# Index tables stored as rows, transfers around a branch respaced, and the last three batches stored in natural row order

## The chip, the cores and the metric

The kernel runs on one core of a Trainium2 chip. The metric is the device time of one execution in microseconds (us), where lower is better. The time before the change is the median of three executions without the profiler; the profile is one further execution with it.

## The reference

Two layers of a graph network act on 32 batches of 512 nodes with 512 features each, all in float32. One 512x512 matrix `adj` serves all batches.

```
h = max(layernorm(x), 0)
x = x + (adj @ h) @ W0 + b0                                        # layer 0
h = max(layernorm(x), 0)
q, k, v = h@Wq+bq, h@Wk+bk, h@Wv+bv                                # layer 1, 8 heads of 64
scores = q k^T / 8 + (1 - adj) * -1e9
x = x + (softmax(scores) v) @ Wo + bo
```

The term of -1e9 outweighs the scores, so when the largest entry of a row of `adj` leads by enough, the softmax takes one neighbour only: layer 1 becomes `x[n] + (h[idx[n]] @ Wv + bv) @ Wo + bo`, where `idx[n]` is the column of the largest entry. The kernel tests for this on the chip and takes this path.

## The kernel before, in words

**Work of one batch.** A tile of x holds 512 rows as four chunks of 128 partitions. Layer 0 is an aggregation (`aggregate`) and a product with W0 (`layer0`). Layer 1 needs only the rows that some `idx` names (at most 336 of 512): the normalised rows h1 are written to a DRAM table `hs` (`put_h`), come back in packed order (`get_h` into `hc`), are multiplied by the folded weight `wvo` (`layer1`), and the result z goes to a DRAM table `z` (`put_z`). Each node then gathers its row of z and adds it to x (`finish`, an indirect DMA that accumulates), and x is stored (`store`). Large products use the seven-piece scheme in `product`, line 506 being the matmul of every piece.

**Loop and order.** `run_phase` walks over b and writes its order by hand. In loop b TensorE runs `layer0(b)`, `aggregate(b+1)` and `layer1(b-1)`; between their pieces lie 21 numbered steps, and `put(batch, step, f, ...)` hangs all other work on a step. Steps 0 to 6 belong to `layer0`, 7 to 13 to `aggregate`, 14 to 20 to `layer1`. Every engine executes its own instructions in this order. `behind` makes each indirect DMA wait until the piece before it has been taken out of PSUM.

**Queues.** Plain DMAs are issued by SyncE (SP). Every indirect DMA, gather or scatter, is issued by GpSimd (POOL). Both feed the same 16 DMA engines.

**The plan and the branch.** While loops 0 to 3 run with a full aggregation, the class `Plan` works out on the chip an order of the rows in which most of the matrix is zero in known blocks. Its steps are in `Plan.schedule`, at (loop, step). After loop 3 (`FIRST = 4`) a register is loaded from its result and all engines branch; on the path taken (`sparse`) rows of x are loaded in the new order through the index table `plan.xi`, `aggregate` becomes `spread` (matmuls of lines 618, 621 and 624), and 3 x 128 extra rows per batch are gathered (`load_g` into `plan.gx`) and normalised into `plan.HG`. That is done by `lead` for the first sparse batch and by `NormMore` (`more_stats`, line 954, and `more_relu`, line 967, on ScalarE) for the others. Rows of the first batches are in natural order (`natural(b)`), so only their `put_h` needs an indirect scatter through `dest` and only their stores are plain. All later stores scatter through `plan.xi` (line 490), each followed by a small memset on POOL (line 493).

**Three small tables in DRAM.** `places` stores `dest` (loop 1, step 0, line 581), `save_pos` stores `posi` (line 1243), `save_pi` stores `pi` (loop 6, step 4, line 1249). Each holds 512 integers that lie on chip as 128 partitions x 4 and are written as

```python
nc.sync.dma_start(table.rearrange("(c p) o -> p (c o)", p=P), dest)
```

so that each integer of 4 bytes is a run of its own in DRAM. Gathers of one integer per partition read them (`look_up`, `look_1`, `look_2`).

**The end.** Batch 31 takes no gather-and-add: `get_all` gathers h1 of every node, and `layer1_rows` transposes it (line 684, copied by ScalarE at line 685) and multiplies it row chunk by row chunk (line 696), adding into x on VectorE (line 699). z of batches 29 and 30 is fetched to spare tiles (`fetch`, into `sel` and `yT`), added on VectorE (`add_z`, line 755) and stored between these. `add_cvo` (line 688) adds the folded bias to batch 31.

Of the kernel before, what the change touches and what calls it, by code (L numbers as in the profile page):

```python
# [408 lines left out]
def single_path(ctx: ExitStack, tc: tile.TileContext, x, adj, out, kept, room):  # L409
# [13 lines left out]
    dest = consts.tile([P, C], I32, name="dest")  # L423
    place = consts.tile([P, C], I32, name="place")
# [12 lines left out]
    hs_d = [dram.tile([N, D], F32, name=f"hs{i}") for i in range(3)]  # L437
    z_d = [dram.tile([32 * S, D], F32, name=f"z{i}") for i in range(3)]
# [16 lines left out]
    def run_phase(batches, sparse, small, ps_m, ps_t):  # L455
        ordered = folded and (sparse or batches[0] == 0)

        def natural(b):
            return not ordered or b <= FIRST

# [25 lines left out]
        def store_rows(b, c, eng):  # L486
            if natural(b):
                eng.dma_start(out[b, c * P:(c + 1) * P, :], X[b][:, c, :])
                return
            stored = behind(nc.gpsimd.indirect_dma_start(  # L490
                out=out_rows, out_offset=bass.IndirectOffsetOnAxis(ap=plan.xi[:, b, c:c + 1], axis=0),
                in_=X[b][:, c, :], in_offset=None))
            nc.gpsimd.memset(gap, 0.0)  # L493
            for other_rows in stored_rows:
                tc.declare_no_dep(stored.ins, other_rows.ins, reason="other rows")
            stored_rows.append(stored)
# [81 lines left out]

        def places():
            table = dram.tile([N, 1], I32, name="table", bufs=1)  # L580
            nc.sync.dma_start(table.rearrange("(c p) o -> p (c o)", p=P), dest)
            return table
# [94 lines left out]
        def get_all(b):  # L677
            for c in range(C):
                gather(hs[0][:, c, :], hs_d[b % 3], idx[:, c, 0:1] if natural(b) else plan.pq[:, c:c + 1])
# [10 lines left out]
        def layer1_rows(b):  # L690
            for r in range(C):
                bank = ps_m.tile([P, D], F32, name="mm")
                for d in range(DC):
                    if d == 2 and r + 1 < C:
                        transpose_all(r + 1)
                    nc.tensor.matmul(bank, hs[1][:, d, r * P:(r + 1) * P], wvo[:, d, :], start=(d == 0),
                                     stop=(d == DC - 1))
                x_r = X[b][:, r, :].rearrange("p (q c e) -> p q c e", q=4, c=4)
                nc.vector.tensor_add(x_r, bank.rearrange("p (c q e) -> p q c e", q=4, c=4), x_r)
                if sparse and r == 0:  # L700
                    for c in range(C):
                        add_z(B - 3, c, nc.sync)
                    fetch(B - 2)
                store_rows(b, r, nc.sync)
                for i in range(2):
                    if not sparse:
                        add_z(B - 3 + r // 2, 2 * (r % 2) + i, nc.sync if r < 2 else nc.scalar)
                    elif 0 < r < C - 1:
                        add_z(B - 2, 2 * r - 2 + i, nc.sync)
# [33 lines left out]
        def place_of(b, c):  # L743
            return (place if natural(b) else plan.place)[:, c:c + 1]
# [5 lines left out]
        def fetch(b):  # L750
            for c in range(C):
                gather(late_z[b][:, c, :], z_d[b % 3], place_of(b, c))
# [22 lines left out]
        for b in batches:  # L775
# [6 lines left out]
            if sparse and b == FIRST:  # L782
                for j in range(3):
                    put(b + 1, 1 + j, lambda b, j: lead.stats(j), j)
                put(b + 1, 3, lambda b: lead.power())
                put(b + 1, 4, lambda b: lead.offset())
                for j in range(3):
                    put(b + 1, 4 + (j + 1) // 2, lambda b, j: lead.relu(j), j)
            if sparse:
                for j, step in enumerate((6, 7, 8) if b == FIRST else (4, 5, 6)):  # L790
                    put(b + 2, step, load_g, [j])
                if last:
                    put(b + 1, 0, lambda b, n=last[-1]: n.offset())
                    for c in range(4):
                        put(b + 1, c, lambda b, c, n=last[-1]: n.relu(c), c)
                    for c in range(3):
                        put(b + 1, 1 + c, lambda b, c, n=last[-1]: n.more_relu(c), c)
# [5 lines left out]
            if b == B - 1:  # L803
                put(b - 2, 15, fetch)
            elif b < B:
                for c, step in enumerate((9, 11, 13, 15) if sparse and b == FIRST else (7, 9, 11, 13) if sparse else
                                         (4, 5, 6, 7) if ordered and b == FIRST - 1 else (1, 2, 3, 4)):
                    put(b - 2, step, finish, [c])
            elif not sparse:
                put(b - 2, 1, fetch)  # L810
# [31 lines left out]
            put(b, 10, put_h, [0, 1] if sparse or b == B - 1 else [0])  # L842
            put(b, 11, lambda b: halves[1].relu(0, b < B - 1))
            if b < B - 1 and not sparse:
                put(b, 11, put_h, [1])
            put(b, 12, lambda b: halves[1].relu(1, b < B - 1))
            put(b, 12, put_h, [2, 3] if sparse or b == B - 1 else [2])
            if b < B - 1 and not sparse:
                put(b, 13, put_h, [3])
            if b < B - 1:  # L850
                if natural(b - 2):
                    put(b - 2, 19 if sparse and b == FIRST else 14 if sparse else 12, store)
                else:
                    for c in range(C):
                        put(b - 2, 14 + 2 * c, store, [c])
            if b < B - 1:
                put(b, 17, get_h)
            else:
                put(b, 13, get_all)
                for c in range(C):  # L860
                    put(b, 15 + c, add_cvo, c)
            for i, step in enumerate((12, 13, 13, 14) if b in (1, B - 1) else (11, 11, 12, 12) if b < B else ()):
# [7 lines left out]
            kind = NormAct if on_act else NormMore if sparse else Norm  # L870
# [4 lines left out]
            else:  # L875
# [3 lines left out]
                if sparse:  # L879
# [11 lines left out]
            if b == 0:  # L891
                put(0, 1, lambda b: number_rows())
                for i in (2, 3):
# [80 lines left out]
class Plan:  # L974
    def __init__(self, tc, consts, dram, adj, kept, upper, B):
# [30 lines left out]
        self.posi = t("posi", [C], I32)  # L1006
        self.off = t("boff", [B, C])
        self.xi, self.gi = t("xi", [B, C], I32), t("gi", [B, 3], I32)
        self.pi, self.pq, self.place, self.pqf = t("pi", [C], I32), t("pq", [C], I32), t("pplace", [C], I32), t("pqf", [C])
# [188 lines left out]
    def positions_3(self):  # L1198
# [3 lines left out]
        v.tensor_copy(self.posi, self.pos)  # L1202
# [39 lines left out]
    def save_pos(self):  # L1242
        self.nc.sync.dma_start(self.posd.rearrange("(c p) o -> p (c o)", p=P), self.posi)
# [4 lines left out]
    def save_pi(self):  # L1248
        self.nc.sync.dma_start(self.tab2.rearrange("(c p) o -> p (c o)", p=P), self.pi)
# [4 lines left out]
    def packed(self):  # L1254
        v = self.nc.vector
        v.tensor_copy(self.pqf, self.pq)
        v.tensor_copy(self.rank, self.pq)
# [3 lines left out]
        v.tensor_copy(self.place, self.pqf)  # L1261
# [23 lines left out]
    def schedule(self):  # L1285
# [36 lines left out]
        at(*divmod(k + 3, 21), self.save_pos)  # L1322
# [11 lines left out]
        move(3, (14, 15, 16, 17), self.tables)  # L1334
# [4 lines left out]
        at(6, 4, self.save_pi)  # L1339
        move(6, (14, 16, 18, 20), self.look_2)  # L1340
        at(7, 5, self.packed)
# [261 lines left out]
```

## Time and profile before

| | |
|---|---|
| time, median of 3 runs | 1025.54 us (1025.52 to 1026.99) |
| profiled execution, its own time | 1038.36 us |
| its span | 1036.5 us |
| TensorE matmuls (PE) | 997.9 us, 96% of the span |
| TensorE weight loads (PEld) | 895.3 us, 86% |
| VectorE (DVE) | 800.1 us, 77% |
| ScalarE (ACT) | 585.8 us, 57% |
| GpSimd (POOL) | 589.1 us, 57% |
| moved by DMA | 204.69 MB, mean 197 GB/s |

The page gives one average for the whole span. A table by stretches of time (busy time of each engine, the granted TensorE clock, the DMA engines' busy share and the rate moved) and lists of one engine's instructions in order of time show how it differs from stage to stage. In those lists an entry's last bracket is the idle time ahead of it and what ended that idle time; "issue" is a time in which the engine waited for no semaphore that the profile shows, "remote" one whose release the profile ascribes to nothing on this core.

### The profile page before, as it was taken

To read this page: it belongs to the slowest core of one execution; us is meant where nothing else is said; L and a number is where in the kernel's file an instruction comes from. 1 tells how busy PE (TensorE), PEld (TensorE's weight loads), DVE (VectorE), ACT (ScalarE), POOL (GpSimd) and SP (SyncE) were. 2 spreads that over 40 slices of the span, in tenths; PEclk is the share of its full clock that TensorE was granted. 3 is DMA by queue.
4 is the path that set the end of the run, shared out by engine and by line. 5 is a ranking of instruction groups with operands and counts; after the bars stand their busy time and mean duration, and the time that the engine had idled before them with its cause. 6 is when DMAs were issued, how large, how long until landed. Compare 5 with 4: busy or idle time off the path is not lost. (4 is left out here: it accounts for less than half of the span.)

```text
span 1036.5 us, 17219 instructions
## 1 busy us (share of the span) xinstructions
PE 997.9 (96%) x5624; PEld 895.3 (86%) x5624; DVE 800.1 (77%) x1779; ACT 585.8 (57%) x1282; POOL 589.1 (57%) x666
## 2 busy tenths in 40 slices
PE   8999989889999999999999999999999999999984
PEld 7477878779999999999999999999999999999872
DVE  5996867668788777888877777788887777778761
ACT  3756353465555566665555556666555555666230
POOL 1033255556656666666666666666666666664436
PEclk9999989989999999999999999999999999999997
DMA  9316488777988888888788888888888888887664
GB/s 315 112 42 159 89 144 237 198 189 198 202 216 216 216 226 218 222 208 201 198 211 216 209 218 228 216 224 202 205 200 210 213 211 218 229 217 186 138 182 162
DMA packets 161140, 204.69 MB, mean 197 GB/s; under 512 B 17873, under 2 KB 105681, under 8 KB 161041
## 3 DMA queue, kind: packets, MB, share of 16 engines
q0 software_dynamic: 44544, 120.10, 48.1%
q1 hardware_dynamic: 115024, 81.99, 29.0%
q10 hardware_dynamic: 1472, 1.41, 0.4%
q8 instruction: 46, 0.75, 0.3%
q14 instruction: 54, 0.43, 0.1%
HBM read 121.45 MB, written 81.99 MB: 196 GB/s over the span
## 5 line engine op out<-in xcount | busy, mean ns | idle before, releaser
L562 DVE TENSOR_TENSOR x<-mm,x 128x512 f32<-128x512 f32 x217 | 148.9, 687 | 137.6 <-PE mm L506 111.0
L473 POOL DMA_INDIRECT x<-z,pplace x96 | 153.4, 1598 | 88.2 <-ACT yT L629 40.9
L379 ACT ACTIVATE h<-x,off,rstd 128x512 f32<-128x512 f32 x256 | 196.0, 804 | 6.2 <-DVE off L370 3.1
L506 PE MATMUL mm<-w_t,sel 128*128 128x256 f32 x744 | 172.4, 381 | 1.3 <-DVE x L562 1.2
L365 ACT ACTIVATE rstd<-mv,eps 128x2 f32<-128x2 f32 (+1 forms) x90 | 26.3, 292 | 245.4 <-DVE mv L362 241.1
L506 PEld LDWEIGHTS mm<-w_t,sel 128*128 128x128 f32 x744 | 141.3, 191 | 21.8 <-DVE x L562 2.4
L361 DVE BATCH_NORM_STATS2 st<-x 128x6 f32<-128x512 f32 x234 | 157.6, 674 | 1.1
L490 POOL DMA_INDIRECT out_dram<-x,xi x108 | 131.8, 1220 | 46.0 <-DVE zs L552 17.7
L621 PE MATMUL mm<-ap,h 128*128 128x256 f32 x648 | 157.7, 380 | 0.0
L473 POOL DMA_INDIRECT x<-in_x_dram,xi x108 | 104.0, 963 | 74.5 <-DVE x L562 26.9
L621 PEld LDWEIGHTS mm<-ap,h 128*128 128x128 f32 x648 | 114.9, 191 | 11.1
L506 PE MATMUL mm<-hTs,wvo_t 128*128 128x168 f32 x720 | 117.9, 314 | 6.1 <-ACT zs L554 5.6
L506 PE MATMUL mm<-w_s,yT 128*128 128x256 f32 x496 | 118.4, 382 | 3.1 <-ACT zs L554 3.1
L473 POOL DMA_INDIRECT at<-in_x_dram,gi x81 | 76.8, 948 | 71.9 <-DVE x L562 22.7
L506 PEld LDWEIGHTS mm<-hTs,wvo_t 128*128 128x128 f32 x720 | 109.2, 195 | 7.2 <-ACT zs L554 6.4
L554 ACT ACTIVATE zs<-mm,cvo_c 128x168 f32<-128x168 f32 x240 | 82.8, 398 | 43.4 <-PE mm L506 25.2
L506 PEld LDWEIGHTS mm<-w_s,yT 128*128 128x128 f32 x496 | 93.3, 191 | 14.9 <-ACT zs L554 3.4
L624 PEld LDWEIGHTS mm<-ag,adjT 128*128 128x128 f32 x648 | 89.3, 191 | 5.6
L624 PE MATMUL mm<-ag,adjT 128*128 128x128 f32 x648 | 89.7, 275 | 0.0
L596 DVE TENSOR_TENSOR x<-x,b_r 128x512 f32<-128x512 f32 x124 | 84.0, 678 | 0.0
L506 PE MATMUL mm<-hT,wvo 128*128 128x168 f32 x480 | 81.2, 314 | 0.0
L629 ACT COPY yT<-mm 128x512 f32<-128x512 f32 x108 | 61.6, 570 | 33.6 <-PE mm L624 29.2
(310 smaller groups left out, 1671.3 us busy)
## 6 DMA issues: line engine op xcount, KB each, us to landing
hc<-hs SPq DMA_DIRECT2D x124, 176.0 KB
z<-zr SPq DMA_DIRECT2D x120, 96.0 KB
hs<-h SPq DMA_DIRECT2D x52, 192.0 KB
z<-zr SPq DMA_DIRECT2D x120, 80.0 KB
hs<-h SPq DMA_DIRECT2D x52, 160.0 KB
out_dram<-x SPq DMA_DIRECT2D x20, 256.0 KB
x<-in_x_dram SPq DMA_DIRECT2D x12, 256.0 KB
x<-in_x_dram,xi POOLq DMA_INDIRECT x108
```

The lines of the kernel that those rows point to most:

```text
L361: self.nc.vector.bn_stats(st, self.src[:, self.chunks[i], :])
L365: self.nc.scalar.activation(self.rstd[:, 0:len(self.chunks)], self.mv[:, :, 1], AF.Sqrt, bias=self.eps)
L379: self.nc.scalar.activation(dst, src, AF.Relu, bias=self.off[:, i:i + 1], scale=self.rstd[:, i:i + 1])
L473: return behind(nc.gpsimd.indirect_dma_start(out=dst, out_offset=None, in_=rows, in_offset=bass.IndirectOffsetOnAxis(ap=at, axis=0), **more))
L490: stored = behind(nc.gpsimd.indirect_dma_start(out=out_rows, out_offset=bass.IndirectOffsetOnAxis(ap=plan.xi[:, b, c:c + 1], axis=0), in_= ...
L506: nc.tensor.matmul(bank[:, m, 0:half], lhs[:, k, m * P:(m + 1) * P], rhs[:, k, :], start=(first and m == 0 and k == 0), stop=(k == 1), ski ...
L554: taken = nc.scalar.activation(dst[:, m, :], bank[:, m, :], AF.Identity, bias=cvo_c[:, 2 * i + m:2 * i + m + 1])
L562: return nc.vector.tensor_add(dst, bank, dst)
L596: nc.vector.tensor_add(X[b][:, c, :], X[b][:, c, :], b0_r)
L621: nc.tensor.matmul(two(bank, j), H0[b][:, j, cols], two(plan.ap[:, j, :], j), start=False, stop=False, skip_group_check=True)
L624: nc.tensor.matmul(bank[:, j * P:(j + 1) * P], extra[:, j - 1, cols], plan.ag[:, j - 1, j * P:(j + 1) * P], start=False, stop=(j == C - 1) ...
L629: tick(nc.scalar.copy(yT[:, d, :], bank))
```

## The change

**Tables.** Each table is first turned into 4 partitions x 128 by a TensorE transpose through PSUM and a VectorE copy to integers (`dest_rows`, `row_pe`, `row_save`), and is stored as four runs of 512 bytes. The stores stay on SyncE. `save_pos` moves two steps later.

**Around the branch.** The four scatters of `put_h` for natural batches move from steps 10, 11, 12, 13 (or 10, 10, 12, 12 in loop 4) to 10, 12, 14, 16, and `get_h` behind them from 17 to 20. The gathers `tables` of loop 3 move from 14 to 17 to 11, 13, 15, 17. In loop 4 `load_g` moves from 6, 7, 8 to 15, 17, 19, `finish` from 9 to 15 to 7 to 13, and `store` from 19 to 18; loop 5 takes over the steps that loop 4 had. `lead` now serves the first two sparse batches, so its statistics for batch 6 are taken in loop 5 in place of `more_stats` in loop 4.

**The last three batches.** x of batches 29, 30 and 31, after layer 0, is scattered to a DRAM table `xn` in natural row order (`turn_back`, four indirect DMAs and memsets on POOL per batch) and loaded back into the same tile (`come_back`, four plain DMAs on SP per batch). Their z is then fetched through `plan.home`, and they are stored by plain DMAs on SP. `plan.home` is a second run of `packed`, in loop 8. `get_all` and `fetch` are split over steps, and `add_cvo` moves from loop 31 into `layer1_rows`, ahead of each addition.

```diff
+        def back(b):
+            return sparse and ordered and b >= B - 3
+        def turn_back(b, chunks):
+            for c in chunks:
+                stored = behind(nc.gpsimd.indirect_dma_start(
+                    out=xn_d[b % 3], out_offset=bass.IndirectOffsetOnAxis(ap=plan.xi[:, 0, c:c + 1], axis=0),
+                    in_=X[b][:, c, :], in_offset=None))
+                nc.gpsimd.memset(gap, 0.0)
...
+        def come_back(b):
+            for c in range(C):
+                load = nc.sync.dma_start(X[b][:, c, :], xn_d[b % 3][c * P:(c + 1) * P, :])
...
-            if natural(b):
+            if natural(b) or back(b):
                 eng.dma_start(out[b, c * P:(c + 1) * P, :], X[b][:, c, :])
...
+        def dest_rows():
+            pt = ps_t.tile([P, DC, P], F32, name="pt")
+            nc.tensor.transpose(pt[0:C, 0, :], pos, ident)
+            nc.vector.tensor_copy(dest_r, pt[0:C, 0, :])
...
-            nc.sync.dma_start(table.rearrange("(c p) o -> p (c o)", p=P), dest)
+            nc.sync.dma_start(table.rearrange("(c p) o -> c (p o)", p=P), dest_r)
...
+                if sparse:
+                    add_cvo(b, r)
...
-            return (place if natural(b) else plan.place)[:, c:c + 1]
+            return (place if natural(b) else plan.home if back(b) else plan.place)[:, c:c + 1]
...
-            if sparse and b == FIRST:
+            if sparse and b <= FIRST + 1:
                 for j in range(3):
                     put(b + 1, 1 + j, lambda b, j: lead.stats(j), j)
...
-                for j, step in enumerate((6, 7, 8) if b == FIRST else (4, 5, 6)):
+                for j, step in enumerate((15, 17, 19) if b == FIRST else (6, 7, 8) if b == FIRST + 1 else (4, 5, 6)):
                     put(b + 2, step, load_g, [j])
...
-                put(b - 2, 15, fetch)
+                for c in range(C):
+                    put(b - 2, 17 + c if sparse else 15, fetch, [c])
...
-            put(b, 10, put_h, [0, 1] if sparse or b == B - 1 else [0])
+            several = b == B - 1 or not natural(b)
+            put(b, 10, put_h, [0, 1] if several else [0])
...
+                for c in range(1, C):
+                    put(b, 10 + 2 * c, put_h, [c])
...
-                put(b, 17, get_h)
+                put(b, 20 if not several else 17, get_h)
...
+            elif b == B - 1:
+                for c in range(C):
+                    put(b, 13 + c, get_all, [c])
+                    put(b, 7 + c, turn_back, [c])
+                    put(b - 1, 2 * c, turn_back, [c])
+                put(b - 1, 8, come_back)
+                put(b, 15, come_back)
+            if sparse and b == B - 2:
+                for c in range(C):
+                    put(b - 1, c, turn_back, [c])
+                put(b - 1, 9, come_back)
...
-            kind = NormAct if on_act else NormMore if sparse else Norm
+            kind = NormAct if on_act else NormMore if sparse and b > FIRST else Norm
...
+    def row_pe(self, ps_t, src):
+        self.ps_r = ps_t.tile([P, 4, P], F32, name="pt")
+        self.nc.tensor.transpose(self.ps_r[0:self.C, 0, :], src, self.kept["ident"])
+    def row_save(self, table):
+        self.nc.vector.tensor_copy(self.prow, self.ps_r[0:self.C, 0, :])
+        self.nc.sync.dma_start(table.rearrange("(c p) o -> c (p o)", p=P), self.prow)
...
-        move(3, (14, 15, 16, 17), self.tables)
+        move(3, (11, 13, 15, 17), self.tables)
...
-        at(7, 5, self.packed)
+        at(7, 5, self.packed, self.pq, self.place)
+        at(8, 5, self.packed, self.pi, self.home)
```

## The prediction

> **What bounds the kernel now.** I read the page's busy shares first: PE 96%. In the table by stretches PE is busy for the whole of each stretch from 234 to 962 us at clock 1.00, so nothing that the change does to POOL, SP or the other engines in there can shorten it. What can be gained lies before 234 and after 988. The list of TensorE's instructions shows four gaps before 234, each followed by matmuls at half the granted clock:
>
> ```profile
> 101.57 0.55 PE L1118 MATMUL pt<-u,at 128*128 128x3 bf16 x16 [2.12 <-DVE u L1130]
> ...
> 142.47 0.16 PE L1224 MATMUL pt<-pc,ph 128*128 128x2 bf16 x1 [1.95 <-issue]
> 144.48 2.61 PE L506 MATMUL mm<-hTs,wvo_t 128*128 128x168 f32 x8 [0.75 <-ACT zs L554]
> 146.88 2.45 PE L506 MATMUL mm<-hT,wvo 128*128 128x168 f32 x8
> ...
> 190.80 3.12 PE L506 MATMUL mm<-w_s,yT 128*128 128x256 f32 x8 [3.15 <-ACT zs L554]
> ...
> 221.19 2.61 PE L506 MATMUL mm<-hTs,wvo_t 128*128 128x168 f32 x8 [4.51 <-ACT zs L554]
> ```
>
> The reader sees the idle time in the bracket and a piece of 8 matmuls that takes 2.61 us where it later takes 1.30. Priced as idle plus start-to-start distance above the normal one (1.14 us for 168 columns, 1.73 for 256):
> - gap 1 at 99.4: 2.12+0.34 idle, then 2.15 and 1.91 between pieces: 4.2 us
> - gap 2 at 139.2: 1.20+1.95+0.55+0.75 idle, then 2.40, 2.24, 1.85: 7.5 us
> - gap 3 at 187.7, the branch: 3.15 idle, then 2.92 for one piece and 4.05 for two: 4.9 us
> - gap 4 at 214.6 to 221.2: 0.41+4.51 idle, then 2.40 and 2.15: 7.2 us
>
> Together 23.8 us. Who is late? The waits of these windows name ScalarE and VectorE, which themselves wait for nothing on the core:
>
> ```profile
> DVE ub L1129 <- remote: 4.6, 1, 4.6
> ...
> ACT zs L554 <- remote: 3.3, 1, 3.3
> ```
>
> For gap 2 the table by single microseconds (last columns: clock, DMA busy share, GB/s) shows the cause. SP stores the table at 129.5; from then to 140 the DMA engines move almost nothing, though stores and scatters are queued; then the backlog runs off at 371 to 428 GB/s:
>
> ```profile
> 129.51 0.38 SPq L1243 DMA_DIRECT2D posd<-posi  x1
> ...
> 133.00:134.00 1.00, 1.00 (x6) 0.87 (x6) 1.00 (x3) 1.00 (x4) 0.87 (x2) 1.00 1.58 8
> ...
> 137.00:138.00 1.00, 1.00 (x9) 1.00 (x8) 1.00 (x3) 0.66 (x2) 0.65 (x1) 1.00 0.33 6
> ...
> 141.00:142.00 1.00, 0.00 (x0) 0.10 (x1) 0.00 (x0) 0.00 (x0) 0.57 (x3) 1.00 1.07 428
> ```
>
> PE then has "issue" ahead of single matmuls: it waits for no semaphore, so I read it as instructions that have not arrived. The other two table stores do the same to the rate: 14 to 51 GB/s from 83 to 90 after the store at 79.05 (POOL waits 14.63 us for its first look-up), and 33 to 68 GB/s from 270 to 276 after the one at 265.48. That one costs PE nothing.
>
> At the end POOL is last. TensorE and VectorE are done 6 us before it:
>
> ```profile
> 1017.26 5.32 PE L696 MATMUL mm<-wvo,h 128*128 128x512 f32 x12
> ...
> 1022.86 0.68 DVE L699 TENSOR_TENSOR x<-mm,x 128x512 f32<-128x512 f32 x1
> ...
> 1028.43 0.96 POOL L490 DMA_INDIRECT out_dram<-x,xi  x1 [0.19 <-issue]
> ```
>
> The chain of waits runs through twelve scatters at 1.27 us start to start and four gathers `yT` between them.
>
> **What the Trainium skill says.** "DMA: Bandwidth & Descriptors", section Specifications: below 512 B a DMA engine does a read-modify-write. The trace agrees in kind: 2 KB in runs of 4 bytes hold the engines for some 10 us. "Runtime: NRT & Kernel Launch", Instruction fetch mechanics: instructions come in blocks of 16 KiB through a DMA queue, and a branch breaks the prefetch. The page's queue q8, kind "instruction", has 46 packets and 0.75 MB, 16 KB each: agreed. "TensorE: Matmul & The Clock Gate", What's actually happening: after an idle window the array runs at half clock. The 2.61 us piece agrees.
>
> **The change, part by part.**
>
> *Tables.* Three stores become four runs of 512 B. Added: three PE transposes, one each (four of line 1269 take 0.60 us, so 0.15, 0.45 together), three VectorE copies and one cast, of 0.17 to 0.29 us, less one cast of 0.17. VectorE is busy 20.6 of 26 us in the steady stage: nothing, and PE pays 0.3 us at most where it was full. The second `packed` is 9 small VectorE operations of 0.17, 1.5 us, in the same slack. Gap 2 loses its cause; I credit 7.0 of 7.5. Gap 1 follows the first table: the look-ups, held to 89.7, push the four scatters of batch 1 to 94.8 to 99.9, on top of the instruction fetches. With the table early and the scatters at steps 10, 12, 14, 16 I credit 2.0 of 4.2, because no line names its cause.
>
> *Around the branch.* In loop 4 POOL issues without a pause from 204.6 to 223.4: three `load_g`, four accumulating `finish`, four scatters. `load_g` to steps 15, 17, 19 and `finish` two steps earlier interleave them one per step. ScalarE's `more_stats` (line 954, which waits 1.60 us for "remote" at 218.26 and holds VectorE for 4.38) leaves loop 4; gap 4 loses 5.0 of 7.2. In exchange `lead` adds 4.5 us of ScalarE (192.58 to 197.1 in loop 4 now) to the start of loop 5. There ScalarE has 4 + 3 relu of 0.8 from 229.4 on: 0.7+3.0+4.5+2.2 ends at about 239.8, and TensorE's first use of `HG` is at 242.77. Cover of 3 us, so nothing; were it gone, TensorE waits 1 to 2 us. Gap 3 keeps the branch itself; the four `tables` gathers start three steps earlier, so I credit 1.5 of 4.9. `get_h` at step 20 waits for the last scatter (step 16, 4 x 1.14 = 4.6 us before) and holds `put_z` behind it on SP; the transposes that need `hc` are at step 5 of the next loop, over 10 us on: nothing.
>
> *The end.* Twelve scatters leave POOL's tail, twelve plain stores go to SP (four took 1.93 us at 130.0, so 0.48 each), and `fetch` of batch 30 no longer stands behind four scatters. The last addition ends at 1023.54, its store is issued by 1024.0 instead of 1029.4: 5.4 us. Added: 12 scatters to `xn` with memsets (1.27 us each, 15.2 us of POOL) and 12 loads (6.3 MB both ways). Batch 29's fall in POOL's idle 951 to 963.85 and a DMA share of 0.44 to 0.02; batch 30's follow the stores that end at 978.6; batch 31's lie at 985 to 991, where DMA is at 0.02. But 3 MB then fall between 985 and 1003. The idle 8 us from 982 take 2.1 MB at 270 GB/s; of the last 1 MB (3.9 us), some 2 us fit in the 20% that 990 to 1002 leave idle, and I charge 2 us to `put_h`, `get_all` and `put_z` of batch 30, hence to TensorE's last stage. On SP `come_back` of batch 31 stands ahead of `put_z` of batch 30, which is ready at 1000.8; its scatters should land by 994. The moved `add_cvo` (4 x 0.68) lies under matmuls. Credit 3.4. No trace of before shows these scatters together with `put_h`: the charge is between 0 (all in the gaps) and 7.2 us (2.1 MB at 290 GB/s, all in series), and I take 2.
>
> Sum against the profiled execution: 7.0+2.0+5.0+1.5+3.4 = 18.9, so 1038.36 becomes 1019.5. The median is 12.8 us below that execution, and the page doesn't say where. PE-bound stages cannot differ, so I put half of it, 6.4, into these gaps and the end (23.8+5.4 = 29.2): they are 22% smaller unprofiled. 18.9 x 0.78 = 14.7; predicted **1011.0 us**.
>
> **The rivals.**
> - *Only the table stall goes.* Late instructions come from block boundaries that happen to meet DMA traffic, and move elsewhere as code moves. For it: gaps 1, 3 and 4 have no named cause. Against: gap 4 sits in the densest run of POOL. 7.0 x 0.78 + 3 = 8.5: 1017. Chance 0.20.
> - *The gaps are a product of profiling*, all 12.8 us and more; only the end counts. 3.5: 1022. Against: the table stall is on the DMA engines. Chance 0.07.
> - *Slower: the detour of x makes DMA the bound of loop 31.* Batches 30 and 31 add 4.2 MB to about 5 MB in 970 to 1000; 9.2 MB at the 290 to 390 GB/s seen at best need 24 to 32 us of 30. If scatters and loads run at 200 GB/s instead, 46 us, `put_h` and `put_z` slip by some 10 us while the end saves 5.4 and the branch nothing: about +4.5, 1030. It decides when TensorE's last stage slips by more than 5.4 plus the branch's gain. Chance 0.09.
> - *The change doesn't do what it says*: four runs of 512 B still clog, or the scatters were the cause. Against: 270 to 276 has no scatter to `hs`. It ends near no change. Chance 0.04.
>
> **How the numbers follow.** The main case has 0.60. Everything gained, 29.2 x 0.78 = 22.8, gives 1003; the profiling rival 1022. Range 1002 to 1022. A measurement of this kernel tells about 0.2%, 2 us, from no change. Faster 0.87 (main and two rivals), same 0.04, slower 0.09.
>
> **What would show it.** Right: no microsecond below 60 GB/s after the table stores; look-ups by 85 us; no "issue" ahead of line 1224; PE without gaps of 4 us between 200 and 230; no line 490 after 985; the last instruction an SP store within 2 us of the last addition. Wrong: TensorE starting its last stage (line 696) 5 us later against `layer1(30)`, waits of `put_z` behind `come_back`, or new gaps of 3 us with "remote" elsewhere.

## The result, and the profile after

| | before | changed | changed / before |
|---|---|---|---|
| first measurement, median | 1025.52 us (1023.77 to 1026.99) | 1018.25 us (1016.82 to 1020.06) | 0.9925 [0.9903, 0.9947] |
| its profiled execution, own time | 1038.36 us | 1019.28 us | |

The changed kernel is 7.3 us faster. Its profiled execution is 19.1 us below that of the kernel before. These two figures are the riddle of this case: the profiled execution was forecast at 1019.5 and came out at 1019.28, the median was forecast at 1011.0 and came out at 1018.25.

The page after, busy shares and the chain that ended last (by engine, in shares of the span). POOL, with 2% the largest part of the chain before, stands at 0%.

```profile
PE 990.3 (97%) x5627; PEld 888.4 (87%) x5627; DVE 801.1 (79%) x1792; ACT 585.5 (58%) x1282; POOL 589.7 (58%) x666
...
PE 75%; DMA 5%; DVE 2%; ACT 2%; issue 1%; POOL 0%; SPq 0%; POOLq 0%; DVEq 0%
```

The stretch of the second table, from the list of instructions. The store is at 130.03, and the matmuls that had "issue" ahead of them follow one another without a pause:

```profile
130.03 0.26 SPq L1291 DMA_DIRECT2D posd<-prow  x1
...
135.75 0.54 PE L1267 MATMUL pt<-pc,ph 128*128 128x2 bf16 x16
...
136.45 1.39 PE L528 MATMUL mm<-hTs,wvo_t 128*128 128x168 f32 x8
```

The same in the table by single microseconds (last columns: clock, DMA busy share, GB/s), after the first store at 79.14 and after the second:

```profile
83.00:84.00 1.00, 1.00 (x7) 0.87 (x6) 0.35 (x2) 0.00 (x0) 0.22 (x1) 1.00 0.99 369
...
133.00:134.00 1.00, 1.00 (x7) 0.92 (x7) 1.00 (x3) 0.97 (x5) 1.00 (x1) 1.00 1.03 387
```

The same microseconds moved 21 and 8 GB/s before; the first of them, before:

```profile
83.00:84.00 1.00, 1.00 (x13) 0.83 (x12) 0.23 (x1) 0.97 (x3) 0.00 (x0) 1.00 0.46 21
```

This agrees with what "DMA: Bandwidth & Descriptors" of the Trainium skill, Specifications, says of pieces below 512 B, that they are read, modified and written back and miss the full rate. The 2 KB are the same, but two things changed at once: the runs grew from 4 to 512 bytes and their number fell from 512 to 4. No run here separates size from number, or shows the read-modify-write itself.

Around the branch and in loop 5, TensorE's list shows where it still waits. Gap 4 is gone from loop 4, and a new one stands one loop later. The granted clock is 0.50 from 236 to 238, and the piece behind the wait takes 2.61 us, twice the 1.30 of later ones:

```profile
178.39 1.99 PE L528 MATMUL mm<-w_s,yT 128*128 128x256 f32 x8 [0.78 <-ACT zs L576]
...
190.51 1.99 PE L528 MATMUL mm<-w_t,yT 128*128 128x256 f32 x8 [1.49 <-DVE x L584]
...
232.10 1.38 PE L528 MATMUL mm<-hTs,wvo_t 128*128 128x168 f32 x8 [0.70 <-DVE hTs L341]
...
235.54 2.61 PE L528 MATMUL mm<-hTs,wvo_t 128*128 128x168 f32 x8 [2.06 <-ACT zs L576]
```

What was late is seen on SP, VectorE and ScalarE. The packed rows `hc` are asked for at 213.65, their first transpose stands 3.71 us on VectorE, and ScalarE then stands 4.96 us for VectorE's next result:

```profile
213.65 1.85 SPq L699 DMA_DIRECT2D hc<-hs  x4
...
223.17 0.71 DVE L752 STREAM_TRANSPOSE hT<-hc 128x512 f32<-128x512 f32 x1 [3.71 <-DMA hc<-hs]
...
226.23 0.29 ACT L365 ACTIVATE rstd<-mv,eps 128x2 f32<-128x2 f32 x1 [4.96 <-DVE mv L362]
```

The end, from the lists of PE, SP and VectorE. TensorE now waits for the gathered rows of batch 31 ahead of line 711, the stores leave on SP, and the last one is issued right behind the last addition:

```profile
988.79 1.11 PE L711 MATMUL pt<-ident,h 128*128 128x128 f32 x4 [4.81 <-DMA h<-hs,pi]
...
997.83 14.54 SPq L510 DMA_DIRECT2D out_dram<-x  x12
...
1011.32 0.69 DVE L728 TENSOR_TENSOR x<-mm,x 128x512 f32<-128x512 f32 x1
```

**A ladder for all kernels.** VectorE's first transpose `hT<-hc` of each batch (line 729 before, 752 after) marks the progress. Its start, in us, in the profile of each kernel told of below, with the chip that it ran on (for the first two it is not known, and it need not be the same one):

```
                       batch 0      1      2      3      4      5      6      8     29     end
before, first profile     88.2  121.0  162.7  202.0  238.6  267.4  296.2  354.2  959.5  1036.5
changed, first profile    89.9  118.0  151.9  190.4  223.2  252.3  281.2  339.6  944.8  1017.5
e1 before      chip 0     88.8  123.4  165.3  205.6  242.8  271.7  300.6  358.5  963.8  1040.9
e2 tables      chip 0     89.5  118.1  152.1  189.2  226.0  254.8  283.7  341.7  946.9  1024.1
e3 respaced    chip 0     88.2  119.0  160.0  201.8  235.3  262.9  296.8  354.9  960.1  1039.8
e4 put back    chip 0     87.6  122.0  163.8  201.7  237.9  266.7  295.6  353.9  959.7  1032.4
e5 changed     chip 10    89.6  117.8  151.7  193.1  226.1  253.7  286.7  345.0  950.9  1024.6
e6 early put   chip 10    91.7  120.1  154.0  194.1  226.2  253.8  284.3  342.7  947.9  1021.6
e7 late back   chip 10    89.8  118.1  152.0  191.6  223.0  252.5  282.4  340.8  946.3  1018.8
e8 2nd table   chip 10    89.0  121.6  155.5  192.5  229.1  258.0  286.9  344.9  950.5  1027.1
e10 both       chip 11    89.6  117.7  151.6  189.7  223.3  250.9  279.8  338.1  943.4  1014.8
e12 changed    chip 11    90.8  119.0  152.8  191.3  224.3  253.6  282.5  340.8  946.0  1019.2
e9 no respacing chip 11   89.0  117.1  151.0  186.9  215.1  245.0  273.2  331.5  936.7  1009.8
e11 late too   chip 11    88.9  117.1  150.9  185.9  214.7  245.1  273.4  332.0  937.2  1008.3
```

From batch 8 to batch 29 all take 605.2 to 605.9 us. Everything is decided ahead of batch 8 and after batch 29. Two profiles of one program can differ there by some us too: the changed kernel takes 129.3, 135.0 and 129.6 us from batch 2 to 6 in its three profiles. From before to changed in the first profiles the steps gain: -1.7 up to batch 0, 4.7 from 0 to 1, 7.8 from 1 to 2, 0.8 from 2 to 3, 3.8 from 3 to 4, -0.7 from 4 to 29, 4.3 at the end; sum 19.0.

### The profile page after: what moved, and what is told of

Read it like the earlier page. It is cut to its first block, busy times and chain, and to the rows that moved or that the text cites. A ratio compares the mean times of both kernels' runs of the same rounds, so it can differ in the third digit from the quotient of the medians.

```text
span 1017.5 us, 17277 instructions
## 1 busy us (share of the span) xinstructions
PE 990.3 (97%) x5627; PEld 888.4 (87%) x5627; DVE 801.1 (79%) x1792; ACT 585.5 (58%) x1282; POOL 589.7 (58%) x666
## 4 chain that ended last, share of the span: by engine, by line
PE 75%; DMA 5%; DVE 2%; ACT 2%; issue 1%; POOL 0%; SPq 0%; POOLq 0%; DVEq 0%
PE mm L528 53%; PE mm L648 13%; PE mm L651 7%; PE mm L645 2%; DMA z<-hc 1%; DMA hc<-hs 1%; DMA at<-in_x_dram,gi 1%; DMA ap<-in_adj_dram,xi 1%; DMA yT<-z,phome 1%; DMA z<-zr 1%; ACT h L379 1%; DMA hs<-h,dest 0%; ACT yT L656 0%; DMA x<-xn 0%; ACT ph L394 0%
## 5 line engine op out<-in xcount | busy, mean ns | idle before, releaser
L512 POOL DMA_INDIRECT out_dram<-x,xi x96 | 120.4, 1254 | 37.3 <-DVE zs L574 20.8
L528 PE MATMUL mm<-hTs,wvo_t 128*128 128x168 f32 x720 | 115.0, 309 | 2.9 <-ACT zs L576 2.1
L528 PEld LDWEIGHTS mm<-hTs,wvo_t 128*128 128x128 f32 x720 | 106.5, 192 | 3.9 <-ACT zs L576 3.0
L528 PE MATMUL mm<-hT,wvo 128*128 128x168 f32 x480 | 78.6, 307 | 0.0
```

Source lines behind the costliest of these rows:

```text
L512: stored = behind(nc.gpsimd.indirect_dma_start(out=out_rows, out_offset=bass.IndirectOffsetOnAxis(ap=plan.xi[:, b, c:c + 1], axis=0), in_= ...
L528: nc.tensor.matmul(bank[:, m, 0:half], lhs[:, k, m * P:(m + 1) * P], rhs[:, k, :], start=(first and m == 0 and k == 0), stop=(k == 1), ski ...
```

## The experiments

The theory was the forecast's own: each part removes its gap, and the gains add. The rival was that stalls only move, so that one part carries nearly everything. Then it turned out that the kernel before takes another time on other chips, and this became a question of its own.

**The kernel before again.** No edit.

> The kernel before, unchanged, profiled once more. If its four gaps before 234 us (23.8 us in the first profile) are a fixed property of the program, this profile again has a span of about 1036 us. If they depend on the moment (the first profile's own time lies 12.8 us above the median, where the changed kernel's profile lies 1 us above its own), the span is nearer 1024 us and some of the gaps are missing or smaller: then the sum of 18.9 us was right for that one profile and half of it was never in the ordinary time. Ratio to the kernel before: 1.000 either way.

On this chip it took 1043.04 us (ratio 1.0008 [0.9991, 1.0025] to the runs of the same kernel beside it, median 1041.75), the profiled execution 1042.62. All four gaps are in the profile; the first and the last of them:

```profile
103.01 0.59 PE L1118 MATMUL pt<-u,at 128*128 128x3 bf16 x16 [2.16 <-DVE u L1130]
...
226.04 2.33 PE L506 MATMUL mm<-hTs,wvo_t 128*128 128x168 f32 x7 [5.02 <-ACT zs L554]
```

So the gaps are not a product of profiling, at least on this chip: here the profiled execution and the median agree within 0.5 us. But here the kernel takes 16 us more than in the first measurement, and the first profile (1038.36) is like this chip, not like the 1025.5 that it was set beside.

**Tables alone.**

```diff
-            nc.sync.dma_start(table.rearrange("(c p) o -> p (c o)", p=P), dest)
+            nc.sync.dma_start(table.rearrange("(c p) o -> c (p o)", p=P), dest_r)
```

(with the transposes and copies ahead of it, and the same in `save_pos` and `save_pi`)

> The kernel before with the three tables stored as rows and nothing else. Theory of the table stall: gap 2 (7.5 us in the first profile) goes in every execution, ratio 0.993 to 0.996 (4 to 7 us). Rival, that the gaps come from instruction blocks that meet any dense traffic: the rate collapse after the stores goes, but TensorE waits elsewhere, ratio 0.998 to 1.001.

1027.11 us, ratio 0.9869 [0.9826, 0.9912]: 14.6 us below the kernel before on that chip. In its profile TensorE has no wait of over 0.2 us between 98 and 150: gap 1 is gone with gap 2. Gap 4 stays (4.83 us). The gain is more than twice the 4 to 7 us expected: against e1 the ladder gives 5.9 us from batch 0 to 1, 7.9 from 1 to 2 and 3.2 from 2 to 3, and only gap 2 was expected.

**The respacing alone.**

```diff
-            put(b, 10, put_h, [0, 1] if sparse or b == B - 1 else [0])
+            put(b, 10, put_h, [0, 1] if several else [0])
...
+                    put(b, 10 + 2 * c, put_h, [c])
...
-                put(b, 17, get_h)
+                put(b, 20 if not several else 17, get_h)
```

(with the moved `load_g`, `finish`, `store`, `tables` and `lead` as in the change)

> The kernel before with the transfers around the branch respaced and nothing else; tables stored element by element, scattered stores at the end. Theory: gap 4 in loop 4 goes, but a gap of 4 to 5 us appears in loop 5, because the packed rows of batch 4 (hc from hs, now loaded at step 20 behind slow stores) land late and hold VectorE: ratio 0.998 to 1.003. Rival, my prediction: gaps 1, 3 and 4 shrink by 8.5 us with nothing in return, ratio 0.992 to 0.995.

1038.69 us, ratio 0.9966 [0.9949, 0.9984]: 3.1 us below. The ladder against e1 says where: 3.8 us between batches 0 and 1 (gap 1), 3.7 between 3 and 4 (gap 4), and 3.7 given back between 4 and 6. The time lies between the two forecasts, and so does the mechanism: the gap comes back as the theory had it, and gap 1 shrinks as the rival had it. Its stalls of loops 5 and 6 in TensorE's list:

```profile
247.64 1.41 PE L506 MATMUL mm<-hTs,wvo_t 128*128 128x168 f32 x8 [1.73 <-ACT zs L554]
...
279.20 1.58 PE L506 MATMUL mm<-hTs,wvo_t 128*128 128x168 f32 x8 [2.48 <-ACT zs L554]
```

So the gain at gap 4 was moved, not made, and the gain at gap 1 is one that the tables bring as well. In this profile 1.6 us are also lost at the branch (batch 2 to 3) and 2.6 behind batch 29, where nothing was edited.

**The last three batches alone.**

```diff
-            if natural(b):
+            if natural(b) or back(b):
...
+                put(b - 1, 8, come_back)
+                put(b, 15, come_back)
```

(with `turn_back`, `home`, the split `fetch` and `get_all`, and the moved `add_cvo`)

> The kernel before with x of the last three batches put back into natural rows and stored by SP, nothing else. From the start of layer1 of batch 30 to the end of the span the kernel before took 44.8 us and the changed one 40.5 us. Theory: this part alone brings 3 to 5 us, ratio 0.995 to 0.997. Rival (the detour makes DMA the bound of loop 31): TensorE's wait of 4.8 us ahead of line 711 in the changed kernel eats it, ratio 0.999 to 1.003.

1036.51 us, ratio 0.9954 [0.9931, 0.9976]: 5.2 us below, a little more than the 3 to 5 us of the theory. Its four gaps are all there.

**The changed kernel on another chip.** No edit.

> The changed kernel, unchanged, on a chip where the kernel before is slow or not, as it comes. The three parts alone gave -14.6, -3.1 and -5.2 us where the kernel before took 1041.75 us; if they add up, the change brings 22 to 23 us there, ratio 0.978, and the 7.3 us of the first measurement belong to a chip on which the kernel before has smaller gaps. If the parts fight each other (loop 5, DMA in loop 31), the ratio is 0.983 to 0.993 where the kernel before takes about 1041 us.

1023.6 us, ratio 0.9812 [0.9793, 0.983]: 19.2 us below a kernel before that took 1042.83 there. The three parts sum to 14.6+3.1+5.2 = 22.9 (on chip 0), so they do not add, though the ratio is lower than what was expected for parts that fight each other; tables and end alone would be 19.8.

**The second and third table as rows, the first as before.**

```diff
-        self.nc.sync.dma_start(self.posd.rearrange("(c p) o -> p (c o)", p=P), self.posi)
+        self.nc.sync.dma_start(table.rearrange("(c p) o -> c (p o)", p=P), self.prow)
```

> The kernel before with only the second and third table stored as rows; the first, of loop 1, element by element as before. Theory: gap 2 goes (7.5 us) and gap 1 stays, because it follows from the first table: two thirds of what all three tables bring on the same chip. Rival: gap 1 has nothing to do with the first table, and this run equals the one with all three.

1029.89 us, ratio 0.9884 [0.9867, 0.99]: 12.9 us below. Gap 2 is gone and gap 1 is there again:

```profile
102.12 0.55 PE L1124 MATMUL pt<-u,at 128*128 128x3 bf16 x16 [1.64 <-DVE u L1136]
```

Gap 1 therefore belongs to the first table, and gap 2 to the second (the third, changed with it, is stored only in loop 6). The first table is not the whole of gap 1: in e3, with the table as before, the moved scatters took 3.8 us of it away. The gain is nearer to that of all three tables (14.6 us on chip 0) than the two thirds expected.

**The scatters of batch 4 one step apart instead of two.** Added to the changed kernel:

```diff
-                    put(b, 10 + 2 * c, put_h, [c])
+                    put(b, 10 + (c if b == FIRST else 2 * c), put_h, [c])
```

> The changed kernel with one size changed: in loop 4 the four put_h at steps 10, 11, 12, 13 instead of 10, 12, 14, 16; get_h stays at 20. Theory: hc of batch 4 lands 4 us earlier, VectorE's wait of 3.71 us at line 752 in loop 5 goes and with it TensorE's gap there (4.8 us in the profile of the changed kernel): 2 to 4 us below the changed kernel. Rival (the gap in loop 5 is due to ScalarE, which now has lead's statistics there): no change against it, within 1 us.

1020.97 us (1017.05 to 1027.22), ratio to before 0.9793 [0.9744, 0.9841]. This tells nothing against e5: the interval is wide, and the next kernel, whose edit acts at batch 30 only, was 4.2 us ahead of e5 at batch 6 as well. In its profile the transpose of `hc` stands 1.31 us for the load and starts 32.1 us after batch 3's mark, in e5 33.0, in e7 31.4; the 4 us of the theory are not there.

**Batch 30's x loaded later.** Added to the changed kernel:

```diff
-                put(b - 1, 8, come_back)
...
+            if sparse and b == B:
+                put(b - 2, 1, come_back)
```

> The changed kernel with come_back of batch 30 moved from loop 31 step 8 behind put_z of batch 30 (it is needed only by the last additions). Theory: 1 MB leaves the stretch in which turn_back of 31, put_h of 31 and put_z of 29 share the DMA engines at 364 to 391 GB/s, so the rows of h1 come 2.7 us earlier, TensorE's wait of 4.81 us ahead of line 711 shrinks to about 2 and the run is 2 to 4 us below the changed kernel. Rival (the wait is for z of batch 29 or for POOL, not for bandwidth): no change, or slower by the later loads.

1020.04 us (1018.57 to 1022.34), ratio to before 0.9785 [0.9764, 0.9806], 3.6 us below e5 by the medians. TensorE's wait ahead of line 711 fell (4.92 us in e5), and one of 3.27 us came later:

```profile
987.43 0.66 PE L711 MATMUL pt<-ident,h 128*128 128x128 f32 x4 [0.55 <-issue]
...
996.83 1.99 PE L723 MATMUL mm<-wvo,h 128*128 128x512 f32 x4 [3.27 <-ACT h L712]
```

Of the 5.8 us between the two spans (1024.6 and 1018.8) 4.5 lie ahead of batch 29, where nothing was edited. In these two profiles the edit itself is worth the rest, 1.3 us.

**No respacing, and the changed kernel beside it.** The tables and the end stay; the calls around the branch go back to their old steps:

```diff
-                put(b, 20 if not several else 17, get_h)
+                put(b, 17, get_h)
...
-                for j, step in enumerate((15, 17, 19) if b == FIRST else (6, 7, 8) if b == FIRST + 1 else (4, 5, 6)):
+                for j, step in enumerate((6, 7, 8) if b == FIRST else (4, 5, 6)):
```

(and `put_h`, `finish`, `store`, `lead`, `tables` likewise)

> The changed kernel with the respacing around the branch taken out: the tables stored as rows and the last three batches put back and stored by SP stay, and the calls around the branch stand in loops 3, 4 and 5 as in the kernel before. Theory 'the parts overlap': with the tables alone the branch's gap and the gap of loop 4 already shrank, and the respacing only moves the remaining stall from loop 4 to loop 5, so it is worth nothing here: the time is that of the changed kernel within 2 us (tables 14.6 and stores 5.2 add up to 19.8 us below the kernel before, where the changed kernel is 19.2 below), and the profile shows a stall of 4 to 5 us in loop 4 and none over 2 us in loops 5 and 6. Rival 'the parts add': the respacing is worth the 3.1 us that it brought alone, and the time is 3 us above the changed kernel's, 16 us below the kernel before.

> The changed kernel once more, so that the three others are compared with it on one chip. In the first measurement it stood 7.3 us below the kernel before, which took 1025.5 us there; where the kernel before took 1042.8 us it stood 19.2 us below. Theory 'the gain is the size of the gaps that the kernel before has on the chip': if the kernel before takes about 1026 us here, the changed kernel stands 6 to 9 us below it; if it takes about 1042, 17 to 21 us. Rival 'the gain is a constant and the first figure was a stray': 18 to 20 us below in both cases.

On this chip the kernel before took 1027.24 us. The changed kernel took 1019.95 us, ratio 0.9932 [0.9905, 0.9959]: 7.3 us below, as in the first measurement, so the gain goes with the time that the kernel before takes on the chip, as the theory of e12 had it. Without the respacing it took 1012.12 us (1011.06 to 1012.89), ratio 0.9846 [0.982, 0.9873]: **15.1 us below**. The respacing costs 7.8 us here. Both theories of e9 fall, and so does its forecast of a stall of 4 to 5 us in loop 4: from 95 to 300 us its whole list of waits on PE is

```profile
176.40 1.99 PE L528 MATMUL mm<-w_s,yT 128*128 128x256 f32 x8 [0.78 <-ACT zs L576]
287.10 1.41 PE L528 MATMUL mm<-hTs,wvo_t 128*128 128x168 f32 x8 [0.41 <-ACT zs L576]
```

while the changed kernel on the same chip has

```profile
191.41 1.99 PE L528 MATMUL mm<-w_t,yT 128*128 128x256 f32 x8 [1.76 <-DVE x L584]
...
233.19 1.38 PE L528 MATMUL mm<-hTs,wvo_t 128*128 128x168 f32 x8 [0.65 <-DVE hTs L341]
...
236.63 1.65 PE L528 MATMUL mm<-hTs,wvo_t 128*128 128x168 f32 x8 [2.06 <-ACT zs L576]
```

The ladder puts 7.5 us between batches 2 and 6 (9.3 at batch 6 less the 1.8 already there at batch 0, at batch 2 still 1.8). Follow `hc` through both, first without the respacing (last scatter to `hs` on POOL, load on SP, first transpose on VectorE):

```profile
202.05 1.47 POOL L688 DMA_INDIRECT hs<-h,dest  x1 [0.19 <-ACT zs L576]
...
205.42 2.48 SPq L699 DMA_DIRECT2D hc<-hs  x4
...
215.09 0.70 DVE L752 STREAM_TRANSPOSE hT<-hc 128x512 f32<-128x512 f32 x1
```

and with it:

```profile
209.51 0.99 POOL L688 DMA_INDIRECT hs<-h,dest  x1 [0.30 <-issue]
...
214.78 1.85 SPq L699 DMA_DIRECT2D hc<-hs  x4
...
224.26 0.71 DVE L752 STREAM_TRANSPOSE hT<-hc 128x512 f32<-128x512 f32 x1 [3.66 <-DMA hc<-hs]
```

Counted from the mark of batch 3 (186.9 and 191.3), the load is issued at 18.5 and at 23.5, and the transpose starts at 28.2 and at 33.0: 4.8 us later, on the path, as the wait for the DMA says. Each load goes out within 0.15 us of the landing of the last scatter (at 205.27 and 214.64), so it is the scatter that holds it, more than the step of `get_h`: of the 5 us, 3.1 come from the scatter's later issue and 1.9 from its longer way to landing (3.2 and 5.1 us). The step before it, from batch 2 to 3, is 2.6 us longer: there too `get_h` at step 20 holds `put_z` on SP (it starts at 180.16 instead of 176.05), its transfers fall on the gathers of the branch, and ScalarE waits 3.88 and 2.26 us for two of those (without the respacing once, 4.66 us), VectorE for ScalarE, and TensorE 1.76 us for VectorE. That the respacing as a whole costs 7.8 us is measured; that the late scatters and `get_h` behind them carry it is read from these lines; no run moved `get_h` alone, and e6 and e10, which move the scatters of batch 4 alone, do not show it.

**The two mends, with and without the respacing.** e10 is the changed kernel with the edits of e6 and e7; e11 is e9 with the edit of e7.

> The changed kernel with both mends at once: the last two scatters of batch 4's features sent two steps earlier, and batch 30's x put back behind the scatter of z of batch 29. Theory: the two sit 700 us apart and share nothing, so what each gave (2.6 and 3.6 us below the changed kernel) adds: 5 to 6 us below the changed kernel, 24 to 26 us below the kernel before in this job, and the profile shows line 711 without its wait of 4.9 us. Rival: the gain of the early scatters was within its interval nothing, and only the late put back counts: 3 to 4 us below the changed kernel.

> Tables as rows, the last three batches put back and stored by SP with batch 30's behind the scatter of z of batch 29, and no respacing. If the respacing is worth nothing beside the tables, this stands within 2 us of the changed kernel with the late put back alone (22 to 23 us below the kernel before) and is the simplest version that beats the changed kernel. If the respacing is worth its 3 us, this stands level with the changed kernel, 19 us below the kernel before.

e10: 1017.49 us (1015.22 to 1023.42), ratio 0.9922 [0.9883, 0.996], 2.5 us below the changed kernel, with ranges that overlap; half of what was expected. In its profile POOL issues the last scatter of batch 4 only 1.3 us earlier than in e12, counted from batch 3's mark, and the rows are no earlier for it (the transpose at 33.6 us, in e12 33.0):

```profile
206.63 0.99 POOL L688 DMA_INDIRECT hs<-h,dest  x1 [0.30 <-issue]
...
212.01 1.85 SPq L699 DMA_DIRECT2D hc<-hs  x4
...
223.26 0.71 DVE L752 STREAM_TRANSPOSE hT<-hc 128x512 f32<-128x512 f32 x1 [3.39 <-DMA z<-zr]
```

While this load was under way, from 212.0 to 223.2, the DMA engines moved 2.81 MB, 1.50 MB of it for POOL's queue, which was fetching x of a later batch. So the wait for the last scatter is not all that makes the rows late. The early scatters are worth nothing that these runs show.

e11: **1009.46 us** (1008.24 to 1012.12), ratio 0.9822 [0.9791, 0.9853], the fastest version here, 10.5 us below the changed kernel; neither forecast had it so fast. From batch 29 to the end e9 takes 73.1 us and e11 71.1, e12 73.2 and e10 71.4, so the late load of batch 30 is worth 1.8 to 2.0 us in these profiles. The medians of e9 and e11 lie 2.7 us apart, with ranges that overlap.

**The same calls on two chips.** Up to loop 8 e2 and e9 have the same calls at the same steps, and yet e2 is 10.2 us behind there, 8.6 of it between batches 3 and 4. Its list in that stretch:

```profile
204.02 0.59 ACT L635 COPY yT<-mm 128x512 f32<-128x512 f32 x1 [3.13 <-PE mm L507]
...
206.30 0.63 ACT L961 ACTIVATE adjT<-at 128x512 f32<-128x512 f32 x1 [1.69 <-DMA hs<-h,dest]
...
208.93 0.65 PE L507 MATMUL mm<-hTs,wvo_t 128*128 128x168 f32 x1 [4.83 <-ACT zs L555]
```

The copy on ScalarE needs a product whose matmuls ended at 200.7 (0.83 us from 199.89), 3.3 us earlier; TensorE then waits for ScalarE. In e9 the same copies follow without a pause. The profile puts ScalarE's wait down to a later matmul of line 507, which this copy does not read; what it really waits for is not shown. Late instructions are a candidate, and no run tested it.

## Why the prediction was right or wrong

The direction was right and the range held the time. The predicted median was 7 us too low: 14.7 us were forecast (1025.5 less 14.7 is 1010.8, written as 1011.0) and 7.3 came.

- **The respacing is the part that failed.** On chip 11 the whole change brings the same 7.3 us as in the first measurement, and without the respacing it brings 15.1. The forecast gave gaps 3 and 4, which the respacing was to close, 6.5 us (5.1 after the factor of 0.78 that converts the profile's gains to the median's) and put `get_h` at step 20 at nothing; measured there, the respacing costs 7.8. Tables and end, credited with 12.4 us (9.7 after the factor), bring 15.1 there. So two errors of opposite sign partly cancel. With 9.7 us for tables and end as forecast and 7.8 lost, the time would be 1023.6, outside the range: that the range held is luck in part.
- **The conversion to the median rests on a spread that does not hold.** Half of the 12.8 us between the first profile and the median was spread evenly over all gaps and the end, so that 78% of each gain would be left. The steady stage cannot have held the rest, since it is the same in every profile. For tables and end the share left was about right: 15.1 us on chip 11 against 14.6+5.2 on chip 0, 76%. Gaps 3 and 4 do not shrink by 22%: in e9, without the respacing, gap 4 is not there and 0.78 us of idle time are left at the branch. They were priced at 12.1 us together, near the 12.8; but where the kernel before takes 1025 to 1027 us no profile of it was taken, so which of its gaps are missing there stays open. The stated alternative, that profiling makes the gaps, falls with e1. The first profile and the first median have the kernel in common, probably not the chip: 1038.36 lies among what chip 0 gave (1036.35 to 1050.63 us) and outside what the first measurement gave (1023.77 to 1026.99).
- **That the profiled sum came within 0.3 us (1019.28 for 1019.5) is luck in good part.** Set against the steps of the ladder, gap 1 brought 2.7 us more than credited, gaps 2 and the end 0.8 and 0.9 more; gaps 3 and 4 brought 0.7 and 1.2 less, and 2.4 were lost up to batch 0 and behind batch 4. Also, these steps set two profiles against each other that probably come from different chips.
- **Pricing by idle time.** "Idle plus slow pieces" fits the first profile, but the slow pieces do not follow from the idle time alone: at the branch the kernel before stood 3.15 us and then had a clock of 0.50 from 192 to 194, while e4 stood 3.18 us there and kept 1.00. And in the stretch after the second store, read as moving almost nothing until 140, the microsecond from 131 to 132 moved 385 GB/s.
- **Gap 2, credited 7.0:** the step from batch 1 to 2 gained 7.8 (7.9 from e1 to e2, on one chip). Right, and with the right cause; that TensorE's "issue" times were late instructions stays a reading.
- **Gap 1, credited 2.0 of 4.2 for want of a named cause:** gained 4.7, all of it (5.9 from e1 to e2). The first table is needed for it, as e8 shows, and close scatters make it worse, as e3 shows. The trace of before had the sign: 14 to 51 GB/s for seven microseconds, some ten ahead of it.
- **Gap 3, credited 1.5:** 0.8 gained. The idle time at the branch is 0.78 us on chip 11 and in the first profile after, and 1.69 to 4.41 us in e2, e5, e6, e7 and e8. "The branch itself" was taken as a fixed 3.4 us. It isn't fixed, though "Runtime: NRT & Kernel Launch" of the Trainium skill (Instruction fetch mechanics) lets one expect a cost there; which part of the 0.78 or of the 4.41 us is fetching, no run here shows.
- **Gap 4, credited 5.0:** 3.8 up to batch 4, and 0.7 of it lost again. Here the step that failed is "`get_h` at step 20 ... over 10 us on: nothing". From the load's issue (213.65) to the transpose (223.17) there were indeed 9.5 us, and the transpose still stood 3.71 us for it: the rows landed only at 223.09. The cover was counted in time alone. The load waits for the last scatter, and while it is under way the DMA engines move 2.21 MB, for `put_z` as well, and 1.20 MB of it for POOL's queue, which was fetching x of a later batch. On chip 11, where e9 has no gap 4 to remove, only this cost is left.
- **The statistics of `lead` in loop 5, costed at nothing:** ScalarE is through with them and then stands 4.96 us for VectorE, so in this profile they are not what TensorE waits for. Not tried alone.
- **The end, credited 3.4 with 2 charged for the detour:** 4.3 gained in the profiles, 5.2 (2.5 to 7.2 by the interval of its ratio) by the medians of e4, this part alone. The charge has a visible part: TensorE's 4.81 us ahead of line 711, of which a later load of batch 30 takes back 1.3 to 2.0. The first product of the last stage did slip by 6.1 us against `layer1(30)` (from 8.9 to 15.0 us behind it), the sign of the slower rival; but the last group of products starts 25.4 us behind it, where it had been 25.6, because the wait of 3.66 us that followed before went. `put_z` did not wait behind `come_back`: it starts 8.8 us after `layer1(30)`, before it was 9.2.
- **The sign "no microsecond below 60 GB/s"** was badly chosen: after the first store there are microseconds at 0 to 1 GB/s from 89 to 94, with a busy share of 0.00 to 0.02; low rates with idle engines mean that little was queued. The sign is a low rate with transfers waiting.
- **The rivals.** "Only the table stall goes, the others move elsewhere" (1017) is nearest in number and in kind: part of gap 4 moved to loop 5, and the tables alone brought 14.6 us on chip 0, where all parts together brought 19.2 on chip 10. But gap 1 went too, with the tables.

## What to carry to other kernels

A table of small integers is written as rows of 512 bytes even if that costs a transpose: three stores of 2 KB were worth 14.6 us on one chip where they held up everything behind them. Before spreading transfers out, follow the last one to the load that waits for it and to that load's first reader, and count what else the DMA engines move in between. Then take the spreading out of the finished change and measure that: alone it gained 3.1 us on chip 0, and inside the change it took back half of what the rest had won on chip 11. A profile and a median are compared only after making sure that they belong together; when they differ by more than the runs do, the difference here lay in the stages with gaps, and not in equal shares.

## What the runs showed of the hardware that was not expected

The same kernel took 1025.5 and 1027.2 us in two measurements and 1041.8 and 1042.8 us in two others, on other chips, while 21 batches of the steady stage took the same time to within 0.7 us in every profile. What differed is stalls, not speed: the changed kernel, with fewer stalls, took 1018.3, 1020.0 and 1023.6 us. Each of the four is one measurement, so chip and moment are not separated.

Two waits of TensorE of the same length at the same place, 3.15 and 3.18 us, were followed by a granted clock of 0.50 in one profile and 1.00 in the other.

A store of 2 KB in runs of 4 bytes can hold back far larger transfers: 6 to 8 GB/s in four of the microseconds from 133 to 138 with stores and scatters queued, where the same store in four runs let 387 GB/s through from 133 to 134.
